# Spreading the bulk transfers, fetching step sizes earlier in a unit, and moving a one-column copy from VectorE to GpSimd in a fused convolution and selective-scan kernel

## The chip, the cores and the metric

The kernel runs on one core of one Trainium2 chip. Its time is the device time of one execution in microseconds (us); of several executions the median is given. One further execution was profiled, and every duration of a single instruction comes from that one.

## The reference, cut to what matters

Two layers with residual connections work on 16 images of 64 x 64 positions and 96 channels, all in float32.

- Layer 0 normalizes each image in groups, upsamples it, applies a quadratic two-layer network per position, low-passes and downsamples it, and adds the input.
- Layer 1 normalizes again, projects to 192 channels and a gate, applies a depthwise 3 x 3 convolution with SiLU, and then runs a selective scan in four directions (rows, columns, and both backwards). It ends with a layer norm, the gate, a projection and the residual.

The scan is the heart of it. For each direction, each of 192 channels and each of 16 states:

```
h = exp(dt[..., None] * As[None]) * h + (dt * ut)[..., None] * bt[:, :, None, :]
y = jnp.einsum('bkdn,bkn->bkd', h, ct)
```

## The kernel before, in words

**Units.** The 4096 positions of an image are cut into four chunks of T = 1024. A *step* is one chunk of one pair of directions: four steps forward (pair 0), then four backward (pair 1), so eight steps an image. A step has six *blocks* (`blocks`, 64 channels of one direction, as two halves e = 0 and e = 1 of 32 channels), and a block has NQ = 4 *units* (index `j`), each of four states. 32 channels times 4 states fill 128 partitions. There are 24 units a step, 192 an image and 3072 in all.

**One unit.** The loop of `scan` over `n` (from L916) writes out a fixed order by hand:

- `recur(n, 1, h)` on VectorE: the scan of half e = 1 over 1024 positions (L803 forward, L805 backward), reading the decay `da` and the drive `b` and starting from the column that the chunk before left in `states`.
- `keep(n, 1, ...)` (L807 to L811): copies the last column of the scan, 128 x 1, into the tile `new`, from where the same block of the next chunk takes it. It is skipped in the last chunk of a pair (`st % NT < NT - 1`), that is in steps 3 and 7 of an image.
- `decay(n + 1, 1)` on ScalarE (L788): exp(step size x a) for the next unit's half 1, written to PSUM. It reads the tile `delta` (the step sizes).
- `slot(0)`: a slice of background work, see below.
- GpSimd multiplies the scan by `ct`, in place in `b` (L963). Then `drive(n + 2)` on GpSimd (L794) makes `b` of the unit after next from `dtu` and `bt`, both halves at once.
- `recur(n, 0, h)` on VectorE, `read_out(n - 1)` on TensorE (L827), `slot(1)`, then VectorE multiplies half 0 by `ct` (L972), ScalarE keeps the column of half 0, `decay(n + 1, 0)`, and `slot(2)`.

One unit in five (SHARE = 5, more when `gate` asks for it) is an *odd* one (`odd_here`): its product of half 1 by `ct` is made by VectorE (L954) and its column is copied by ScalarE, so GpSimd has only the drive to do. In this kernel 614 of the 3072 units are odd.

**Loads for the next block.** With `j == 0` both halves of `dtu` for the next block are asked for, with `j == 1` the step sizes of half 1, and with `j == 2`, after `slot(2)`, those of half 0 (`fetch_delta(*ahead, 0)`, three buffers in `sc_3`). Every transfer is issued from SyncE's queue (SP), which is in order: an issue that must wait holds those behind it.

**Background.** Layer 0 and the convolution of the next image (`front`, with its group norm `norm`), the output part of the last image (`finish`), and the projection of the next step (`project`) are generators. A `Background` object takes a slice of one at each `slot` so that `slices` of them are spread evenly over `positions`: SLICES = 499 slices over POS = 576 positions (192 units x 3 slots). A yield counts as one slice, `yield HEAVY` as two. `parts` (L196) loads or stores one whole-image tile in pieces and yields after each: it is used for the image's input, for `made["x1"]`, for `made["xs"][1]`, and for `ycol` in `finish` (six pieces of 512 KB, at the start of step 6 of each image).

Of the kernel before, what the change touches and what calls it, by code (L numbers as in the profile page):

```python
# [68 lines left out]
NEPS = 1e-5  # L69
BOTH = "natural_log_exp_and_others"  # L70
POS = 3 * 8 * 6 * NQ
SLICES = 499
WAIT = -1
BUSY = -2
HEAVY = 2
# [5 lines left out]
def tile_two_blocks(  # L81
# [4 lines left out]
    nc = tc.nc  # L86
# [109 lines left out]
    def parts(out, in_, n=4):  # L196

        step = L // n
        for i in range(n):
            nc.sync.dma_start(out=out[:, step * i:step * i + step], in_=in_[:, step * i:step * i + step])  # L200
            yield

    def norm(xt):

# [418 lines left out]
    def scan():  # L623


        with ExitStack() as es:
# [85 lines left out]
            def spread(out, what, ctx, bi, e):  # L712

                v, s0, r = blocks[bi]
                nc.sync.dma_start(
                    out=out,
                    in_=ctx[what][v][32 * (s0 + e):32 * (s0 + e) + 32, :].unsqueeze(1).to_broadcast([32, NQ, T]),
                )

            def fetch_dtu(ctx, bi):  # L720
                t = p2.tile([128, 2, T], F32, name="dtu")
                for e in range(2):
                    spread(t[:, e, :], "dtu", ctx, bi, e)
                return t

            def fetch_delta(ctx, bi, e):
                t = p3.tile([128, T], F32, name="delta")
                spread(t, "delta", ctx, bi, e)
                return t
# [11 lines left out]
            def fetch_y0(lc, bi):  # L741
                y0 = yp.tile([128, 2 * QT], F32, name="y0")
                nc.sync.dma_start(out=y0, in_=ypart[lc, bi])
                return y0
# [6 lines left out]
            bc, dtus, deltas = {}, {}, {}  # L751
# [33 lines left out]
            def decay(n, e):  # L785
                k, g = group(n, e)
                da = aps.tile([128, T], F32, name="da", tag=f"da{e}")
                nc.scalar.activation(da, deltas[n // NQ, e], AF.Exp, scale=a_s[:, k, g, units[n][2]:units[n][2] + 1])  # L788
                das[n, e] = da

            def drive(n):
                b = p4.tile([128, 2, T], F32, name="b")
                bt = bc[0, blocks[units[n][1]][2], units[n][2]]
                nc.gpsimd.tensor_mul(b, dtus[n // NQ], bt.unsqueeze(1).to_broadcast([128, 2, T]))  # L794
                bs[n] = b

            def recur(n, e, out):
                st, bi, j = units[n]
                pair = steps[st][1]
                da, b = das.pop((n, e)), bs[n][:, e, :]  # L800
                before = 0.0 if st % NT == 0 else states[bi][0][:, e, j:j + 1]
                if pair == 0:
                    nc.vector.tensor_tensor_scan(out, da, b, before, ALU.mult, ALU.add)  # L803
                else:
                    nc.vector.tensor_tensor_scan(out[:, ::-1], da[:, ::-1], b[:, ::-1], before, ALU.mult, ALU.add)  # L805

            def keep(n, e, h, copy):  # L807
                st, bi, j = units[n]
                if st % NT < NT - 1:
                    end = h[:, T - 1:T] if steps[st][1] == 0 else h[:, 0:1]  # L810
                    copy(states[bi][1][:, e, j:j + 1], end)  # L811
# [70 lines left out]
            def slot(position):  # L882
                nonlocal full, full_unit
                back = ahead_gen if ahead_gen.gen is not None else behind_gen
                back.at += 1
                step_gen.at += 1
                gate = back.said == WAIT and back.due() and position == 2 and storing is None
                if gate:
                    full, full_unit = 2, n + 1
                if step_gen.due() and not (full and step_gen.said == BUSY):  # L890
                    light = step_gen.said != BUSY
                    step_gen.step()

                    if light and step_gen.due() and step_gen.said != BUSY:
                        step_gen.step()
                if back.due() and (gate or back.said != WAIT):
                    back.step()
                full = max(full - 1, 0)

            last = len(units) - 1  # L900
            def next_step(st, mi):

                nonlocal step_gen
                if st < len(steps):
                    if steps[st][0] > mi:
                        ahead_gen.drain()
                    step_gen = Background(project(*steps[st], ctxs[st], gps), PSLICES, 3 * per_step)
# [8 lines left out]
            for n, (st, bi, j) in enumerate(units):  # L916
                mi, pair, lc = steps[st]
                v, s0, r = blocks[bi]
                m = n // NQ
                if n % per_image == 0:  # L920
                    image[mi]["y"] = dram.tile([2, DI, L], F32, name="y_d")
                    behind_gen.drain()
                    ahead_gen = behind_gen = nothing
                    if mi + 1 < B:
                        ahead_gen = Background(front(mi + 1), SLICES, POS)
                elif n % per_image == 2 and mi > 0:
                    behind_gen = Background(finish(mi - 1), SLICES, POS)
                if j == 0:
                    new = stp.tile([128, 2, NQ], F32, name="new", tag=f"st{bi}")
                    states[bi] = (states[bi][1] if states[bi] else None, new)  # L930

                if j == 0:
                    ahead = None
                    if bi + 1 < len(blocks):
                        ahead = ctxs[st], bi + 1
                    elif n + NQ <= last:
                        step_gen.drain()
                        ahead = ctxs[st + 1], 0
                        next_step(st + 2, mi)
                    if ahead:  # L940
                        dtus[m + 1] = fetch_dtu(*ahead)
                elif j == 1:
                    if ahead:
                        deltas[m + 1, 1] = fetch_delta(*ahead, 1)


                credit += 1
                odd_here = n == full_unit or credit >= SHARE
                if odd_here:
                    credit -= SHARE  # L950
                h = das[n, 1] if odd_here else bs[n][:, 1, :]
                recur(n, 1, h)
                if odd_here:
                    nc.vector.tensor_mul(bs[n][:, 1, :], h, bc[1, r, j])  # L954
                keep(n, 1, h, nc.scalar.copy if odd_here else nc.vector.tensor_copy)
                if n < last:
                    decay(n + 1, 1)
                slot(0)
                if storing is not None:
                    next(storing, 0)  # L960
                    storing = None
                if not odd_here:
                    nc.gpsimd.tensor_mul(h, h, bc[1, r, j])  # L963
                if n + 2 <= last:
                    drive(n + 2)

                h = das[n, 0]
                recur(n, 0, h)
                if n >= 1:
                    read_out(n - 1)  # L970
                slot(1)
                nc.vector.tensor_mul(bs[n][:, 0, :], h, bc[1, r, j])  # L972
                keep(n, 0, h, nc.scalar.copy)
                if n < last:
                    decay(n + 1, 0)
                if n >= 1 and units[n - 1][2] == NQ - 1:
                    storing = store(n - 1)
                    next(storing)
                slot(2)
                if j == 2 and ahead:  # L980
                    deltas[m + 1, 0] = fetch_delta(*ahead, 0)
                if j == NQ - 1 and n < last and steps[units[n + 1][0]][1] == 1:
                    st2, bi2, _ = units[n + 1]
                    y0s[steps[st2][2], bi2] = fetch_y0(steps[st2][2], bi2)


                at = n % per_step
                for what in range(2):
                    ahead_j = at - (2 * NQ - 1 + what)
                    if 0 <= ahead_j < NQ:  # L990
                        bc[what, 1, ahead_j] = fetch_bc(ctxs[st], 1, ahead_j, what)
                    ahead_j = at - (5 * NQ - 1 + what)
                    if 0 <= ahead_j < NQ and st + 1 < len(steps):
                        bc[what, 0, ahead_j] = fetch_bc(ctxs[st + 1], 0, ahead_j, what)
# [113 lines left out]
```

## Time and profile before

| | |
|---|---|
| median of 3 runs | 21079.41 us (21074.11 to 21098.74) |
| profiled execution | 21085.42 us, of which the span from first to last instruction is 21083.6 us |
| before the first scan (first image's `front`) | about 470 us |
| busy, share of the span | VectorE 93%, GpSimd 92%, TensorE 80%, ScalarE 65% |
| DMA | 203 GB/s in the mean; 1536 step-size loads of 512 KB |
| copies of a last column (L811) | 1844 on VectorE, 2764 on ScalarE |

*Busy* is the union of the times in which an engine executes. Idle time before an instruction is put down to what ended it (its *releaser*). The profile names engines DVE (VectorE), ACT (ScalarE), POOL (GpSimd), PE (TensorE; PEld for its weight loads) and SP (SyncE). [...]

### The profile page before, as it was taken

The page shows a single profiled execution, that of the slowest core. Times are in us where ns is not written, and L with a number is a line of the kernel's source. Part 1 is how long each engine was busy: PE and PEld are TensorE (multiplying, and loading weights), DVE is VectorE, ACT ScalarE, POOL GpSimd, SP SyncE. Part 2 cuts the span into 40 slices and gives each one's busy share as a digit, 9 for nine tenths or more (in the row PEclk, how much of TensorE's full clock was granted, in tenths as well). Part 3 has the DMA queues.
Part 4 walks back from the last instruction along what each step waited for, and adds up shares of the span by engine and source line. Part 5 has one row for each costly group of instructions (what it writes and reads, how often), then busy time and mean ns, then how long its engine had stood idle before and what let it go on. Part 6 is the DMA issues. An engine that isn't in the chain of part 4 may idle for free. (4 is left out here: it accounts for less than half of the span.)

```text
span 21083.6 us, 273452 instructions
## 1 busy us (share of the span) xinstructions
PE 16908.7 (80%) x98988; PEld 7230.6 (34%) x98988; DVE 19569.4 (93%) x12983; ACT 13780.9 (65%) x20546; POOL 19498.8 (92%) x5538
## 2 busy tenths in 40 slices
PE   7876788888878788788788888888787787888856
PEld 4423324233343333324333242333433333243221
DVE  0999999999999999999999999999999999999997
ACT  4666666667666666666666666676666666666553
POOL 0999999999999999999999999999999999999996
PEclk8887888888889888898888988888898888988977
DMA  2565565655656566565665656556565665656654
GB/s 84 191 202 195 195 227 195 221 202 196 226 198 227 197 210 212 194 230 191 218 207 197 226 199 219 202 197 222 197 226 198 212 212 198 229 195 216 224 186 141
DMA packets 1855464, 4277.11 MB, mean 203 GB/s; under 512 B 449438, under 2 KB 548670, under 8 KB 1852062
## 3 DMA queue, kind: packets, MB, share of 16 engines
q1 hardware_dynamic: 1854110, 4259.62, 60.1%
q8 instruction: 781, 12.80, 0.3%
q14 instruction: 573, 4.69, 0.1%
HBM read 3380.58 MB, written 878.18 MB: 202 GB/s over the span
## 5 line engine op out<-in xcount | busy, mean ns | idle before, releaser
L794 POOL TENSOR_TENSOR b<-dtu,bt 128x2048 f32<-128x2048 f32 x3072 | 13895.8, 4532 | 581.2 <-DMA dtu<-dtu_d 465.1
L788 ACT ACTIVATE da<-delta,a_s 128x1024 f32<-128x1024 f32 x6144 | 6857.4, 1117 | 2562.1 <-DVE b L972 945.5
L963 POOL TENSOR_TENSOR b<-b,ct 128x1024 f32<-128x1024 f32 x2458 | 5797.1, 2358 | 836.9 <-DVE new L811 628.6
L827 PE MATMUL y<-b,fold_s 128*32 128x256 f32 x49152 | 3871.3, 437 | 1153.0 <-DVE b L972 680.8
L972 DVE TENSOR_TENSOR b<-da,ct 128x1024 f32<-128x1024 f32 x3072 | 3756.4, 1223 | 91.8
L803 DVE TENSOR_TENSOR_SCAN da<-da,new,b 128x1024 f32<-128x1024 f32 x1383 | 3245.3, 2347 | 72.7 <-ACT da L788 57.2
L805 DVE TENSOR_TENSOR_SCAN da<-da,new,b 128x1024 f32<-128x1024 f32 x1361 | 3193.0, 2346 | 99.7 <-ACT da L788 77.0
L827 PEld LDWEIGHTS y<-b,fold_s 128*32 128x32 f32 x49152 | 1388.5, 119 | 3876.9 <-issue 1464.0
L805 DVE TENSOR_TENSOR_SCAN b<-da,new,b 128x1024 f32<-128x1024 f32 x943 | 2208.7, 2342 | 139.3 <-ACT da L788 81.5
L803 DVE TENSOR_TENSOR_SCAN b<-da,new,b 128x1024 f32<-128x1024 f32 x921 | 2156.5, 2341 | 11.2 <-ACT da L788 10.5
L811 ACT COPY new<-da 128x1 f32<-128x1 f32 x2764 | 432.9, 157 | 2607.4 <-DVE b L972 2236.0
L488 PE MATMUL c_ps<-xgp,wtap_s 96*64 96x512 f32 (+1 forms) x4608 | 1728.2, 633 | 184.7 <-ACT row L506 179.4
L697 PE MATMUL s<-w,ident_s 128*128 128x512 f32 x1530 | 1167.2, 854 | 636.0 <-ACT w L692 614.2
L371 PE MATMUL h_ps<-xu,w1t_s 96*128 96x500 f32 x1920 | 1044.0, 643 | 299.9 <-ACT t L311 125.9
L383 PE MATMUL o_ps<-w2c_s,hsq 128*100 128x96 f32 x9600 | 1041.5, 266 | 178.1 <-ACT hsq L352 177.8
L677 PE MATMUL s<-pr,dtw_s 128*128 128x512 f32 x1530 | 928.5, 691 | 315.2 <-ACT delta L703 224.9
L805 DVE TENSOR_TENSOR_SCAN da<-da,b 128x1024 f32<-128x1024 f32 x482 | 1103.5, 2289 | 53.0 <-ACT da L788 43.1
L383 PEld LDWEIGHTS o_ps<-w2c_s,hsq 128*100 128x100 f32 x9600 | 975.0, 179 | 410.3 <-ACT hsq L352 232.1
L803 DVE TENSOR_TENSOR_SCAN da<-da,b 128x1024 f32<-128x1024 f32 x460 | 1053.0, 2289 | 36.8 <-ACT da L788 34.8
L697 PE MATMUL s<-e,ident_s 128*128 128x512 f32 x1530 | 1004.2, 745 | 0.0
L820 PE MATMUL y<-y,ident_s 128*128 128x512 f32 x768 | 524.2, 770 | 583.5 <-ACT yt L838 457.6
L488 PEld LDWEIGHTS c_ps<-xgp,wtap_s 96*64 96x64 f32 (+1 forms) x4608 | 583.1, 169 | 1121.7 <-issue 842.6
(143 smaller groups left out, 21936.5 us busy)
## 6 DMA issues: line engine op xcount, KB each, us to landing
dtu<-dtu_d SPq DMA_DIRECT2D x1536, 512.0 KB
delta<-delta_d SPq DMA_DIRECT2D x1536, 512.0 KB
bt<-rows SPq DMA_DIRECT2D x1024, 512.0 KB
ct<-rows SPq DMA_DIRECT2D x1024, 512.0 KB
u<-xs_d SPq DMA_DIRECT2D x893, 256.0 KB
dtu_d<-dtu SPq DMA_DIRECT2D x765, 256.0 KB
delta_d<-delta SPq DMA_DIRECT2D x765, 256.0 KB
xr<-in_x SPq DMA_DIRECT2D x768, 128.0 KB
```

Of the source, the lines that this page charges most:

```text
L371: nc.tensor.matmul(h_ps[j], lhsT=w1t_s[:, 128 * j:128 * (j + 1)], rhs=xu.rearrange("c p q -> c (p q)"), start=True, stop=True,)
L383: nc.tensor.matmul(o_ps[:, p, :], lhsT=hsq[j][:, UPS * p:UPS * (p + 1)], rhs=w2c_s[:, j, :], start=(j == 0), stop=(j == HB - 1),)
L488: nc.tensor.matmul(c_ps[p:p + n], lhsT=wtap_s[:, tap, 128 * i:128 * i + n], rhs=xgp[:, h0:h0 + 8, dx:dx + HW], start=(tap == 0), stop=(tap ...
L677: nc.tensor.matmul(s, lhsT=dtw_s[:, pair, v, :], rhs=pr, start=True, stop=True)
L697: nc.tensor.matmul(s, lhsT=ident_s, rhs=of, start=(k == 0), stop=(k == 3))
L788: nc.scalar.activation(da, deltas[n // NQ, e], AF.Exp, scale=a_s[:, k, g, units[n][2]:units[n][2] + 1])
L794: nc.gpsimd.tensor_mul(b, dtus[n // NQ], bt.unsqueeze(1).to_broadcast([128, 2, T]))
L803: nc.vector.tensor_tensor_scan(out, da, b, before, ALU.mult, ALU.add)
L805: nc.vector.tensor_tensor_scan(out[:, ::-1], da[:, ::-1], b[:, ::-1], before, ALU.mult, ALU.add)
L827: nc.tensor.matmul(y[32 * q:32 * q + 32, e, :], lhsT=fold_s, rhs=b[:, e, QT * q:QT * q + QT], start=(pair == 0 and j == 0 and e == 0), sto ...
L963: nc.gpsimd.tensor_mul(h, h, bc[1, r, j])
L972: nc.vector.tensor_mul(bs[n][:, 0, :], h, bc[1, r, j])
```

## The change

Four edits:

- `parts` yields HEAVY after each piece instead of a plain yield, so each piece takes two slices of the background's budget.
- SLICES goes from 499 to 517.
- The step sizes of half 0 of the next block are asked for after `slot(0)` of the unit `j == 2` instead of after its `slot(2)`.
- In the units that are not odd, the last column of half 1 is copied by GpSimd instead of VectorE.

```
-SLICES = 499
+SLICES = 517
...
             nc.sync.dma_start(out=out[:, step * i:step * i + step], in_=in_[:, step * i:step * i + step])
-            yield
+            yield HEAVY
...
-                keep(n, 1, h, nc.scalar.copy if odd_here else nc.vector.tensor_copy)
+                keep(n, 1, h, nc.scalar.copy if odd_here else nc.gpsimd.tensor_copy)
                 if n < last:
                     decay(n + 1, 1)
                 slot(0)
+                if j == 2 and ahead:
+                    deltas[m + 1, 0] = fetch_delta(*ahead, 0)
...
                 slot(2)
-                if j == 2 and ahead:
-                    deltas[m + 1, 0] = fetch_delta(*ahead, 0)
```

## The prediction, on record before the changed kernel ran

> **What bounds the kernel now.** I read the busy shares, then the busy times step by step, then who waits for whom.
>
> ```profile
> PE 16908.7 (80%) x98988; PEld 7230.6 (34%) x98988; DVE 19569.4 (93%) x12983; ACT 13780.9 (65%) x20546; POOL 19498.8 (92%) x5538
> ```
>
> VectorE (DVE) and GpSimd (POOL) lie one per cent apart, so the average doesn't say which sets the pace. The busy times of eight windows do, the eight steps of one image (index 10; borders at the first scan of each step). Columns: window, length, busy us (instructions) of each engine, granted clock, DMA share, GB/s.
>
> ```profile
> core 0: us, PE busy (x) PEld busy (x) DVE busy (x) ACT busy (x) POOL busy (x), PEclk, DMA share, GB/s
> 13302.30:13461.50 159.20, 116.30 (x822) 57.10 (x822) 153.12 (x107) 108.14 (x188) 151.14 (x44) 0.77 0.57 189
> 13461.50:13619.30 157.80, 128.73 (x1050) 70.07 (x1043) 151.08 (x104) 109.46 (x173) 152.43 (x44) 0.88 0.59 199
> 13619.30:13773.70 154.40, 127.46 (x1034) 67.41 (x1034) 150.60 (x103) 107.07 (x170) 152.44 (x45) 0.86 0.58 200
> 13773.70:13924.70 151.00, 126.23 (x820) 65.07 (x812) 147.68 (x85) 99.94 (x132) 151.00 (x43) 0.85 0.60 203
> 13924.70:14091.70 167.00, 120.15 (x633) 40.60 (x634) 157.72 (x108) 122.25 (x196) 148.15 (x43) 0.81 0.61 200
> 14091.70:14258.00 166.30, 144.17 (x628) 55.93 (x627) 154.46 (x102) 123.45 (x169) 146.68 (x41) 0.93 0.62 212
> 14258.00:14421.70 163.70, 142.22 (x615) 46.57 (x616) 153.03 (x115) 95.34 (x143) 161.93 (x49) 0.94 0.75 244
> 14421.70:14579.90 158.20, 139.76 (x610) 45.49 (x608) 154.35 (x95) 93.38 (x120) 154.31 (x44) 0.94 0.67 222
> ```
>
> GpSimd's idle time (length less busy) is 8.1, 5.4, 2.0, 0, 18.9, 19.6, 1.8 and 3.9 us. So GpSimd bounds steps 3 and 6; VectorE, with what it waits for, bounds 4 and 5, and by a smaller margin 0, 1 and 2. GpSimd's list of waits (us in total, times, longest) says that most of its idle time ends with the copy that moves. The second line is what the copy's own source line shows (min/median/max ns):
>
> ```profile
> POOL b L963 <- DVE new L811: 628.6, 296, 14.1
> ...
> L811 DVE COPY new<-b x1844: 153/154/157, 496.4 to 20763.7; 128x1 f32<-128x1 f32 x185
> ```
>
> **What the Trainium skill says.**
> - "Perfetto Trace Analysis", GPSIMD Engine Instruction: a GpSimd span is unreliable, and start-to-start spacing is what to use. The trace agrees: neighbours overlap by 0.04 us (below), so I use spacings.
> - "GPSIMD Engine Reference", 2.1 Instruction dispatch: consecutive GpSimd instructions don't wait for each other; one that needs the result of another waits for its semaphore after the write is acknowledged. No row of this trace has such a pair; the change makes 1844 of them.
> - "SBUF — State Buffer", Who interferes with whom: a VectorE instruction with two SBUF inputs contends with a GpSimd instruction that reads SBUF. The trace agrees: the 96 x 1 product of `norm` (L237) takes 156 ns at best and a median of 5728 ns:
>
> ```profile
> L237 DVE TENSOR_TENSOR nb<-nmean,rg x32: 156/5728/12324, 38.7 to 19074.5; 96x1 f32<-96x1 f32 x32
> ```
>
> The copy (one input, 153 to 157 ns each time) doesn't suffer so, hence no such gain comes from moving it.
>
> **The copy leaves VectorE.** The timeline of VectorE, two stretches: with the copy, and in a step without it.
>
> ```profile
> 8000.25 2.35 DVE L805 TENSOR_TENSOR_SCAN b<-da,new,b 128x1024 f32<-128x1024 f32 x1
> 8002.64 0.15 DVE L811 COPY new<-b 128x1 f32<-128x1 f32 x1
> 8002.71 2.35 DVE L805 TENSOR_TENSOR_SCAN da<-da,new,b 128x1024 f32<-128x1024 f32 x1
> ...
> 8020.69 2.35 DVE L805 TENSOR_TENSOR_SCAN b<-da,new,b 128x1024 f32<-128x1024 f32 x1 [0.76 <-POOL b L794]
> 8022.96 2.33 DVE L805 TENSOR_TENSOR_SCAN da<-da,new,b 128x1024 f32<-128x1024 f32 x1
> ```
>
> From scan to scan 2.46 us with it, 2.27 us without: 0.19 us saved per copy, since the copy's wait for the scan goes too. All 1844: 350 us, the most that can be won.
>
> **The copy comes to GpSimd**, between the wait for the scan and the product L963. The product overwrites the column that the copy reads, so it now waits for the copy. Behind both stand the drive of the unit after next and then the next unit's copy; VectorE's scans wait for the drive. GpSimd's timeline:
>
> ```profile
> 8000.16 2.36 POOL L963 TENSOR_TENSOR b<-b,ct 128x1024 f32<-128x1024 f32 x1
> 8002.47 4.54 POOL L794 TENSOR_TENSOR b<-dtu,bt 128x2048 f32<-128x2048 f32 x1
> 8006.97 2.36 POOL L963 TENSOR_TENSOR b<-b,ct 128x1024 f32<-128x1024 f32 x1
> ```
>
> Spacings are 2.31 us for 1024 elements and 4.50 for 2048: (4.50 - 2.31)/1024 = 2.14 ns an element, and 2.31 - 2.19 = 0.12 us is fixed. A one-element copy should cost about the fixed part. The new wait costs the overlap (0.04 us) and the way from end to start, an estimate of 0.08 us: VectorE's copy ended at 14190.48 and GpSimd's product started at 14190.61, 0.13 us later, with which I bound it. So c = 0.24 us a copy; ends 0.12 (the wait is free) and 0.36 (twice the instruction's fixed cost and the dearer wait, rounded).
>
> **Ledger by step.** With k copies in a step (20, 19, 19, 0, 18, 16, 24, 0 in this image), a step changes by the larger of -0.19 k (VectorE's gain) and c k less GpSimd's idle time. At c = 0.24:
> - step 0: 4.8 - 8.1 = -3.3; step 1: 4.6 - 5.4 = -0.8; step 2: 4.6 - 2.0 = +2.6
> - steps 4 and 5: -0.19 x 18 = -3.4 and -0.19 x 16 = -3.0, the idle time is ample
> - step 6: 5.8 - 1.8 = +4.0; steps 3 and 7: nothing is moved
> - sum -3.9 us an image, over 16 images **-62 us**.
>
> At c = 0.12 the same gives -11.9 an image, -190 us; at 0.36 +6.0, +96 us. I take half of the gain of steps 4 and 5 back, +3.2 x 16 = **+51 us**: there VectorE waits for ScalarE's decays (5.8 us in step 5), which needn't come earlier.
>
> **The normalizing product.** L237 took 195 us in all, 12 us an image. Counting yields, it stands in the changed order after another third of its unit (once after `slot(0)` instead of `slot(2)`, once after `slot(1)` instead of `slot(0)`). GpSimd's new pause between copy and product may also let it in sooner. Ends: all but 100 us of it stays, or it grows by 10 us. I take **-2 us x 16 = -32 us**.
>
> **Step sizes sooner.** The load waits for `decay(n + 1, 1)` to free its buffer, and SP often stands there already; only where other issues hold it up does the move help. ScalarE's wait that it can remove, and SP's wait:
>
> ```profile
> ACT da L788 <- DMA delta<-delta_d: 123.9, 56, 5.3
> ...
> SPq L715 <- ACT da L788: 2159.9, 445, 19.8
> ```
>
> Of the 124 us, 102 lie in the first two blocks of step 6, among the six `ycol` pieces, and there GpSimd is the bound: of the scan gaps that they make (about 3.2 us an image), it was idle for less than 1.8 us. All 768 such loads move past SP's issues of slots 1 and 2: stores of results that come later anyway, and background loads, which now wait up to the 3.5 us from scan start to decay end; they are asked for several slots ahead, and without that lead the delay would be theirs in full. **-12 us**, from -45 to +20.
>
> **Spread.** 18 pieces (12 in `front`, 6 in `finish`) take one slice more, and SLICES rises by 18: all other background comes 517/499 = 3.6% denser, ends at the same place, and nothing is added. It hides under the same scans; were the cover gone in steps 4 and 5, 3.6% of the 5 us an image that VectorE waits there would be 3 us in all. Counted at nothing.
>
> **Sum:** -62 + 51 - 32 - 12 = -55 us against the profiled execution (21085.4, of which 21083.6 span). That is 6 us above the median of the runs; the changed kernel should have about 21079 - 55 = 21025.
>
> **Rivals.** What can be told from no change here is about 0.2%, 42 us.
> - *Small gain* (48%): as summed; its own range 20900 to 21037.
> - *No change* (20%): GpSimd gives back in steps 2 and 6 what VectorE gains in 0, 4 and 5. For it: the two are balanced. Time 21060 to 21100. The sooner load doing nothing belongs here: SP waits at it already.
> - *GpSimd becomes the bound* (32%), slower: with c = 0.36, +96 + 51 - 32 - 12 = +103, 21180. The place is steps 1, 2 and 6; the sum changes sign near c = 0.29 and passes 42 us near 0.31. For it: 92% busy and no idle time in step 6; against: 38 us idle in steps 4 and 5.
>
> The range reaches from the cheap copy (-190 + 51 - 44 = -183, 20896) to a little past the dear one: 20900 to 21200.
>
> **What would show it.** Right: L811 on GpSimd x1844, a spacing from copy to product near 0.24; step 6 longer by about 4 us, steps 0, 4 and 5 shorter by 2 to 3; the wait of L963 for VectorE below 350 us; L788's wait for `delta` near zero; VectorE's waits for L794 grown from about 100 us. Wrong: a spacing above 0.3 us, or steps 4 and 5 unchanged.

## The result, and the profile after

The changed kernel takes 21142.44 us (median of 9 runs, 21136.19 to 21147.69), the kernel before in the same comparison 21084.11 us (9 runs). The ratio is 1.0027, 95% interval 1.0018 to 1.0035: **slower by 58 us**, where 55 us less were forecast.

The busy line of its profile:

```profile
PE 16904.3 (80%) x98988; PEld 7135.5 (34%) x98988; DVE 19192.3 (91%) x11139; ACT 13804.2 (65%) x20546; POOL 19811.7 (94%) x7382
```

VectorE is busy for 377 us less (136 of them are L237's, see below) and GpSimd for 313 us more. GpSimd is now the busier one. The windows of the same image (index 10) for steps 0, 4, 5 and 6, same columns as before:

```profile
13327.20:13486.90 159.70, 116.23 (x812) 55.85 (x812) 151.30 (x87) 109.35 (x189) 153.35 (x63) 0.77 0.58 193
...
13953.40:14114.50 161.10, 121.55 (x638) 41.04 (x639) 148.83 (x91) 122.90 (x196) 151.10 (x60) 0.84 0.63 204
14114.50:14282.10 167.60, 142.04 (x625) 55.19 (x624) 152.19 (x87) 123.00 (x170) 147.98 (x57) 0.92 0.62 213
14282.10:14451.40 169.30, 144.99 (x613) 46.21 (x612) 150.16 (x90) 96.44 (x142) 167.38 (x73) 0.92 0.73 236
```

Step 4 went from 167.0 to 161.1 us, step 6 from 163.7 to 169.3, and step 5 got 1.3 us longer, although GpSimd idles there for 19.6 us as before. Two source lines follow, then VectorE's waits for GpSimd's drive L794, first before and then after the change:

```profile
L811 POOL COPY new<-b x1844: 175/185/303, 502.7 to 20824.4; 128x1 f32<-128x1 f32 x185
...
L237 DVE TENSOR_TENSOR nb<-nmean,rg x32: 155/1750/4459, 39.6 to 19111.3; 96x1 f32<-96x1 f32 x32
```

```profile
DVE b L805 <- POOL b L794: 51.9, 92, 0.9
...
DVE da L805 <- POOL b L794: 30.2, 42, 0.9
...
DVE da L803 <- POOL b L794: 14.2, 24, 0.9
...
DVE b L803 <- POOL b L794: 4.9, 6, 2.6
```

```profile
DVE b L805 <- POOL b L794: 343.0, 359, 2.7
...
DVE da L803 <- POOL b L794: 173.9, 215, 1.3
...
DVE b L803 <- POOL b L794: 79.1, 111, 2.8
DVE da L805 <- POOL b L794: 56.1, 69, 1.3
```

Over these four kinds of scan, VectorE now waits 652 us for L794 instead of 101. And the norm's product L237, once 195.0 us in all with a median of 5728 ns, comes down to 59.5 us. The GpSimd timeline in step 6 shows the price of a copy (the product of half 1 by `ct`, L963 before, is L965 in this kernel):

```profile
14305.70 4.53 POOL L794 TENSOR_TENSOR b<-dtu,bt 128x2048 f32<-128x2048 f32 x1
14310.17 0.18 POOL L811 COPY new<-b 128x1 f32<-128x1 f32 x1
14310.44 2.35 POOL L965 TENSOR_TENSOR b<-b,ct 128x1024 f32<-128x1024 f32 x1
14312.75 4.53 POOL L794 TENSOR_TENSOR b<-dtu,bt 128x2048 f32<-128x2048 f32 x1
```

From drive to product it is 14310.44 - 14305.70 = 4.74 us; without a copy 4.49 (median of the trace). So **c = 0.25 us**: the copy's 0.18 to 0.19 us overlaps the drive by 0.06, and the product starts 0.08 us after the copy's end.

### The profile page after: what moved, and what is told of

Read it like the earlier page. It is cut to its first block, busy times and chain, and to the rows that moved or that the text cites. A ratio compares the mean times of both kernels' runs of the same rounds, so it can differ in the third digit from the quotient of the medians.

```text
span 21141.9 us, 274388 instructions
## 1 busy us (share of the span) xinstructions
PE 16904.3 (80%) x98988; PEld 7135.5 (34%) x98988; DVE 19192.3 (91%) x11139; ACT 13804.2 (65%) x20546; POOL 19811.7 (94%) x7382
## 5 line engine op out<-in xcount | busy, mean ns | idle before, releaser
L794 POOL TENSOR_TENSOR b<-dtu,bt 128x2048 f32<-128x2048 f32 x3072 | 13905.2, 4535 | 534.6 <-DMA dtu<-dtu_d 465.4
L965 POOL TENSOR_TENSOR b<-b,ct 128x1024 f32<-128x1024 f32 x2458 | 5799.5, 2359 | 186.0 <-DVE b L805 37.2
L827 PE MATMUL y<-b,fold_s 128*32 128x256 f32 x49152 | 3885.0, 434 | 1530.6 <-DVE b L974 605.7
L827 PEld LDWEIGHTS y<-b,fold_s 128*32 128x32 f32 x49152 | 1344.5, 118 | 4417.3 <-issue 1371.3
L697 PE MATMUL s<-d,ident_s 128*128 128x512 f32 x1530 | 922.1, 689 | 0.0
```

The lines of the kernel that those rows point to most:

```text
L697: nc.tensor.matmul(s, lhsT=ident_s, rhs=of, start=(k == 0), stop=(k == 3))
L827: nc.tensor.matmul(y[32 * q:32 * q + 32, e, :], lhsT=fold_s, rhs=b[:, e, QT * q:QT * q + QT], start=(pair == 0 and j == 0 and e == 0), sto ...
```

## The experiments

Ratios are to the kernel before, run in the same comparison, with the 95% interval. "Step k" differences are sums over the 16 images of a step's length in the profiled execution, from first scan to first scan.

### One edit at a time: e1 to e4

e1 is the kernel before with the copy edit; e2 with SLICES = 517 and HEAVY; e3 with the sooner load; e4 with both of these and without the copy. The diffs are the lines of the change.

> The kernel before with the GpSimd copy as its only edit. Theory A (the copy is the cause: 1844 x 0.25 us more on GpSimd, which is the bound in steps 2, 3 and 6 and is waited for in the others): slower than before by 0.2 to 0.5%, VectorE's waits for the drive L794 grown from about 100 us to 500 us or more. Theory B (the denser background or the sooner load is the cause): faster by 0.2% or no change, since VectorE is rid of 350 us. On the normalizing product L237: if the pause between GpSimd's copy and product lets it in, its total falls from 195 us to about 60 us here; if its new place in the unit does, it stays near 195 us.

> The kernel before with SLICES = 517 and the HEAVY yields only. Theory A: no change beyond 0.1%. Theory B: slower by 0.2% or more. L237: near 195 us in all if the pause after the copy was what shortened it; near 60 us if its place in the unit was.

> The kernel before with the sooner load of half 0's step sizes only. Theory A: within 0.1% of before; ScalarE's wait for delta falls from 124 us to under 40 us, and SyncE's waits before L715 grow or stay. Theory B (SyncE is held at the load and the stores behind it come late): slower by 0.2% or more.

> The changed kernel with the copy put back on VectorE: spread and sooner load together. Theory A: 0 to 0.2% faster than before, so that the copy alone makes the loss of 0.27%. Theory B: as slow as the changed kernel, 21140 us.

Measured: e1 0.9989 (0.9982 to 0.9995), e2 0.9996 (0.9987 to 1.0004), e3 1.0002 (0.9994 to 1.0010), e4 0.9992 (0.9984 to 1.0000). Both theories fall, though theory A had VectorE's wait for L794 right (497 us in e1). No edit alone makes the kernel slower, the copy alone makes it slightly faster, and 1.0027 comes only when they meet. ScalarE's wait for `delta` fell from 124 to 69 us in e3 (under 40 was expected), and to 9 us in the changed kernel; the time did not follow.

The total of L237 settles one point. The source line of L237 in e2 (spread alone) and in e1 (copy alone):

```profile
L237 DVE TENSOR_TENSOR nb<-nmean,rg x32: 155/5990/12969, 38.5 to 19060.3; 96x1 f32<-96x1 f32 x32
```

```profile
L237 DVE TENSOR_TENSOR nb<-nmean,rg x32: 144/1535/4312, 38.6 to 19038.8; 96x1 f32<-96x1 f32 x32
```

In all 211 us and 52 us. The copy shortens it; the new place in the unit only shifts it: summed over the images, L237 in step 4 goes from 122 us before to 81 in e2, but in step 0 from 73 to 130.

### Which edit clashes with the copy: e5 and e6

e5 is e1 with the spread, e6 is e1 with the sooner load.

> The kernel before with the copy on GpSimd and the spread (SLICES = 517, HEAVY yields), the load of the step sizes where it was. Alone the copy gave a ratio of 0.9989 and the spread 0.9996. Theory C (spread and copy don't add: the spread moves VectorE's late moments out of steps 2, 3 and 7, where GpSimd is now the bound and can't use it, and into steps 0 and 5, where it costs): slower than before by 0.2 to 0.3%, as the changed kernel. Theory D (sooner load and copy don't add): as the copy alone, 0.1% faster.

> The kernel before with the copy on GpSimd and the sooner load, no spread. Theory C: as the copy alone, about 0.1% faster than before. Theory D: slower than before by 0.2 to 0.3%.

Measured: e5 1.0026 (1.0016 to 1.0037), e6 0.9991 (0.9983 to 0.9999). It is the spread; the sooner load is out of it. In the profiled executions the copy alone makes -16 us, the spread alone -1 and both +58: 75 us that don't add, of which 40 lie in step 4, 23 in step 5 and 15 in step 0. So the outcome is theory C's, but its reason (costs in steps 0 and 5) leaves out the largest part.

### What a copy on GpSimd costs, and whether order helps: e7 and e8

```
                     copy(states[bi][1][:, e, j:j + 1], end)
+                    if copy == nc.gpsimd.tensor_copy:
+                        copy(states[bi][1][:, e, j:j + 1], end)
```

> The changed kernel with each of the 1844 copies made twice by GpSimd (the second waits for the first, 0.26 us more each). If GpSimd is the bound in steps 0 to 3 and 6 now, as the ledger has it: 82 of 115 copies an image pay in full, 82 x 16 x 0.26 = 340 us, to about 21480 (+1.6% to the changed kernel). If time is set elsewhere (waits for ScalarE and TensorE): below +0.5%.

Measured: 1.0206 (1.0192 to 1.0220), 21523 us. Against the changed kernel that is +381 us for 1844 x 0.26 = 479 us of GpSimd time: 79% of it comes out at the end, more than the 340 us expected. By steps, over nine tenths come out in 1, 2 and 6, two thirds in 0 and 5, and under a third in 4. So a further delay of GpSimd is paid for over most of the scan.

```
                     nc.vector.tensor_mul(bs[n][:, 1, :], h, bc[1, r, j])
+                if n + 2 <= last:
+                    drive(n + 2)
                 keep(n, 1, h, nc.scalar.copy if odd_here else nc.gpsimd.tensor_copy)
...
                     nc.gpsimd.tensor_mul(h, h, bc[1, r, j])
-                if n + 2 <= last:
-                    drive(n + 2)
```

> The changed kernel with the drive of the unit after next issued to GpSimd ahead of the copy and the product of half 1 instead of behind them, so that GpSimd has 4.5 us of work that doesn't wait for VectorE's scan. If the two engines lose time by waiting for each other in turn (VectorE 652 us for L794, GpSimd about 520 us for VectorE): faster than the changed kernel by 1 to 2%. If the drive then waits for the read-out on TensorE to free its buffer: no gain, and the wait of L794 for L827 grows from 42 us to several hundred.

Measured: 1.0031 (1.0019 to 1.0043), no gain. VectorE's wait for L794 did go, from 652 to 31 us, but GpSimd's drive now waits for the read-out L827 on TensorE to free its buffer, 275 us instead of 42, as the rival said (waits of GpSimd in e8; for the second line the profile shows no releaser):

```profile
POOL b L794 <- PE y L827: 274.5, 135, 7.1
POOL b L794 <- issue: 192.9, 97, 4.0
```

VectorE's wait of L702 for TensorE also doubled, from 340 to 657 us. So the mutual waits could be moved and not removed; whether they would vanish with one more buffer of `b` was not tried.

### The stall of the norm's product: e9 and e10

```
-        nc.vector.tensor_mul(nb, nmean, rg)
+        nc.scalar.activation(nb, nmean, AF.Identity, scale=rg)
```

> The kernel before with the 96 x 1 product of the norm (L237, two SBUF inputs) made by ScalarE instead of VectorE. Theory E (VectorE is held for the whole 195 us of L237 by GpSimd's use of SBUF, and steps 0 and 4 can use nearly all of it back): faster than before by 0.5 to 0.9%, steps 0 and 4 together shorter by 9 to 12 us an image. Rival (GpSimd is close behind and takes over as the bound): less than 0.2%.

> The changed kernel with the same edit. Theory E with a copy that costs: what the copy won was mostly L237 (195 to 60 us), so with L237 gone from VectorE in both kernels the copy and the spread together cost 0.7 to 1.0% (150 to 200 us) instead of 0.27%; this kernel is within 0.4% of the changed one and slower than e9 by that much. Rival (L237 has nothing to do with it): it differs from e9 by 0.27%.

Measured: e9 (on the kernel before) 0.9928 (0.9914 to 0.9941), e10 (on the changed one) 1.0000 (0.9992 to 1.0008). Theory E holds for the time: 152 us fewer in e9, from 195 us of stall. (By what VectorE was held, e9 doesn't test; see the last section.) On the changed kernel the same edit wins only 57 us. **With L237 off VectorE the change costs 0.72%, 152 us**; the kernel as measured hides 94 us of that, since L237 is held less in it.

e9 also shows what GpSimd's idle time in step 4 was. Before, in the timelines of VectorE and of GpSimd:

```profile
13960.19 8.18 DVE L237 TENSOR_TENSOR nb<-nmean,rg 96x1 f32<-96x1 f32 x1 [0.23 <-ACT rg L234]
```

```profile
13974.59 2.35 POOL L963 TENSOR_TENSOR b<-b,ct 128x1024 f32<-128x1024 f32 x1 [6.25 <-DVE new L811]
```

VectorE is held for 8.18 us; the next scan is late by that, and GpSimd then idles for 6.25 us. With L237 on ScalarE the window of step 4 is (columns as before):

```profile
13813.80:13971.80 158.00, 119.02 (x633) 40.27 (x634) 149.66 (x107) 122.28 (x197) 148.10 (x43) 0.83 0.65 213
```

GpSimd's idle time in it is 158.0 - 148.1 = 9.9 us instead of 18.9. About half of the idle time of that step, which the prediction called ample, was the shadow of that stall.

### The two-by-two table without the stall: e13 and e14

e13 is e9 with the copy on GpSimd, e14 is e9 with the spread.

> e9 (norm's product on ScalarE) with the GpSimd copy, without the spread. Copy and spread cost 75 us more together than apart while L237 was on VectorE. Theory F (they share one gain: both shorten the same stall of L237 in steps 0 and 4): with L237 away nothing is left to share, so this run and e14 add up to e10 within 30 us; the copy alone costs 110 to 160 us against e9. Rival G (the spread moves the forced odd units, and GpSimd bound by the copies pays for that): the 75 us stay, the copy alone costs about 80 us.

> e9 with the spread, without the copy. Theory F: within 0.2% of e9, slower rather than faster, since its better place for L237 in step 4 (2.5 us an image) is worth nothing now: +10 to +40 us. Rival G: as the spread alone did before, 0 to -10 us.

Measured: e13 0.9973 (0.9962 to 0.9983), e14 0.9934 (0.9922 to 0.9947). Against e9 the copy costs 0.45% (95 us, between what F and G expected), the spread 0.06% (13 us, not clear of noise), both 0.72% (152 us; e10, which stands for both, has the sooner load too, but e5 and the changed kernel, 1.0026 and 1.0027, differ by that alone). What doesn't add has gone from 0.41% to 0.21%. By steps, the 40 us of step 4 are gone (-2 us), while 19 us in step 5 stay. Theory F explains about half: copy and spread each shorten the same stall in step 4 (L237 there: 122 us before, 28 with the copy, 81 with the spread, 17 with both). For the rest, the place speaks for rival G: it lies in the last four units of step 5, after the last odd unit that `gate` forces, which with the spread comes two units earlier (unit 18 instead of 20 in image 10). The intervals leave the size of that part open, and it wasn't tested by itself.

### The copy off GpSimd: e11, e12, e15

```
-                keep(n, 1, h, nc.scalar.copy if odd_here else nc.gpsimd.tensor_copy)
+                keep(n, 1, h, nc.scalar.copy)
```

e11 has this edit on the changed kernel, e12 with that of e9 besides; e15 has both on the kernel before.

> The changed kernel with every copy of a last column on ScalarE, so that VectorE is rid of it as in the changed kernel and GpSimd doesn't get it. Theory A (the load on GpSimd is what costs): faster than the changed kernel by 0.4 to 1.0%, L237 back at about 210 us, VectorE's waits for L794 back below 300 us. Rival (the copy's place between scan and product costs, whoever makes it): not faster than the changed kernel; GpSimd waits for ScalarE's copy by several hundred us.

> The changed kernel with the last columns and the norm's product on ScalarE. If the two gains add: faster than the kernel before by 0.7 to 1.4%. If GpSimd is then the bound nearly everywhere, no more than e9.

> The kernel before with the last columns and the norm's product on ScalarE, without spread and sooner load. If the spread and the sooner load are worth nothing of their own: the same as e12 within 0.1%; if they are worth the 0.08% that they made together, slower than e12 by as much.

Measured: e11 0.9947 (0.9934 to 0.9959), e12 0.9909 (0.9895 to 0.9922), e15 0.9896 (0.9881 to 0.9911). The copy's load on GpSimd is what costs: moved to ScalarE, the same copy wins 0.8% (e11 against the changed kernel), although GpSimd then waits for it, 722 us in e11 and here in e15:

```profile
POOL b L963 <- ACT new L811: 597.8, 331, 14.8
```

About half of the 598 us (291) passes before the end of the scan whose last column is copied; of the 629 us before it was 531. So ScalarE's copy keeps GpSimd waiting longer after the scan than VectorE's did (307 us against 98), and e15 is faster all the same. Two expectations for e11 failed: VectorE's waits for L794 are 387 us, more than 300, and L237 did not go back to 210 us but to 137 in all, with no copy on GpSimd:

```profile
L237 DVE TENSOR_TENSOR nb<-nmean,rg x32: 155/3956/13384, 38.8 to 18964.0; 96x1 f32<-96x1 f32 x32
```

e15, without spread and sooner load, has the lowest time of all, 20863 us, but its interval overlaps that of e12. All that this shows is that the two edits win nothing there.

## Why the prediction was wrong

Step by step, in us over 16 images (forecast: the ledger of the one image times 16, with half of the gain in steps 4 and 5 taken back; copy alone: e13 less e9, where L237 doesn't blur it):

| step | 0 | 1 | 2 | 3 | 4 | 5 | 6 | 7 | sum |
|---|---|---|---|---|---|---|---|---|---|
| ledger of the copy, forecast | -53 | -13 | +42 | 0 | -27 | -24 | +64 | 0 | -11 |
| copy alone, e13 less e9 | -42 | 0 | +22 | +29 | +19 | -21 | +84 | +9 | +100 |
| whole change, measured | -27 | -4 | +32 | +18 | -68 | +17 | +95 | -5 | +58 |

- **The price of a copy was right**: 0.25 us for the 0.24 forecast, and 0.19 us saved on VectorE.
- **The step that failed is the ledger by step**: it forecast -11 us, and the copy alone made +100 in the profiled executions (+95 by the ratios). It let the idle time that GpSimd has anywhere in a step pay for the copies of that step. The largest miss (46 us) is its term "the idle time is ample" in step 4: half of that idle time followed L237, and the rest lies in a few units, while the copies come in others where GpSimd has none. In e13 GpSimd still idles 8.8 us in step 4 of image 10 (159.7 - 150.9), and yet VectorE waits for it; the waits of that window show it (first GpSimd's, then VectorE's, shown below). The same ledger from the trace of before, over all 16 images with c = 0.254, gives -12 us over steps of 24 units, +17 over 12, +82 over six and +141 over four. So shorter stretches turn its sign, but the sum depends on their length, and with six it misses the gain in step 0 (+21 for -42).
- **One image stood for 16.** With c = 0.24, all 16 images give -28 us where image 10 times 16 gave -62, and +20 instead of -11 with the half taken back. So some 31 of the 111 us come from the choice of the image.
- **"Steps 3 and 7: nothing is moved" failed** in step 3, by 29 us. No copy is made there, but the extra lies in its first eight units: GpSimd, the bound there, enters it late from step 2. Its drive ends 1.9 us before the first scan of the step that reads it in e9 and 0.35 us before it in e13 (means of the images), and this lost lead is made up over those units.
- **Step 6** was forecast too low (+64 for +84): GpSimd's idle time in it is 1.3 us in the mean of the images before, not the 1.8 of image 10, and it seems that not all of it could be used.
- **The normalizing product** was undersized: 94 us came back and not 32. The copy was the cause, as e1 and e2 show, and for it I had no price; but the pause between copy and product, which I named as possible, is not where L237 got in (last section).
- **"Spread, counted at nothing"** held for the spread alone (0.9996) and failed beside the copy, where it costs 57 us without L237 (e10 less e13) and 78 us with it (e5 less e1).
- **"Step sizes sooner", -12 us,** came out as nothing: 1.0002 alone. Beside copy and spread it took ScalarE's wait for `delta` from 65 us (e5) to 9 (the changed kernel) at the same time, so that wait had been hidden.

The waits of step 4 of image 10 in e13, GpSimd's and VectorE's (us in total, times, longest):

```profile
POOL new L811 <- DVE b L805: 5.7, 2, 2.9
```

```profile
DVE da L805 <- POOL b L794: 2.2, 3, 1.3
...
DVE b L805 <- POOL b L794: 1.8, 3, 0.9
```

GpSimd's idle time is two waits and a third for TensorE; in six other places VectorE waits for GpSimd.

Put together from the runs: copy +95, spread beside it +57 (152 in all without L237), less 94 for L237: +58. Of the rivals, *GpSimd becomes the bound* was the one that came true, in steps 2 and 6 as described, in step 3 instead of 1, and with c at 0.25, where the ledger still promised a gain. Most of the signs of being right came although the forecast was wrong, so they did not tell the two apart: VectorE's waits for L794 grew sixfold, and step 6 grew by 5.9 us an image (95/16). Two did not come: step 5 got longer, and GpSimd's waits for VectorE's scan before its copy are 442 us, not below 350.

## What to carry to other kernels

When two engines are within a per cent of each other, idle time of one, added up over a long stage, need not be room for more work: look in which few microseconds it lies, and whether it is the shadow of the other's stall. Make such a ledger over several lengths of stretch and over the whole run; where its sign depends on them, as here, it can't carry a forecast. And look first for an instruction that takes more than 30 times its best time: moving one 96 x 1 product won 152 us, where the whole change lost 58.

## What was not expected of the hardware

- A one-column copy on GpSimd that the next instruction waits for takes 0.25 us of its queue, though it moves one element in each partition: 0.185 us of span and 0.08 us until the product starts, less 0.06 us of overlap with the drive before it; and the 0.04 us by which product and drive overlapped without it are lost.
- In the scan of the kernel before, VectorE's L237 was not let in between GpSimd instructions that follow each other closely: all 30 times its hold ended within 0.02 us of the end of a drive after which GpSimd had run out of work, at most 12.3 us later and over three instructions that had started meanwhile. "SBUF — State Buffer" of the Trainium skill (Summary: rules for kernel authors) has the later one of two such instructions blocked until the earlier one is through; here it was blocked for up to three more.
- With the copies on GpSimd the longest hold was 4.5 us, and in 26 of 30 cases it ended where one GpSimd instruction gave way to the next with no pause between them (drive to copy, product to drive, drive to drive), in only three between copy and product. In e11, with the copies on ScalarE, 13 of 30 holds ended between a drive and a product too. Why L237 is let in at such a place in these kernels and not in the one before, the runs don't show.
